# Low-rank inputs of an FFN folded into a redundant row of the quarter sums and into VectorE, with the next block's tokens turned between chunks

## The chip, the core and the metric

One core of a Trainium2 chip runs the whole program. The metric is the device time of one launch in microseconds (us). Before the change it is 2009.09 us, the median of three runs (2008.93 to 2010.6).

## What is computed

All tensors are float32. With x of shape (8, 256, 512), that is 2048 tokens of width 512:

```python
xn  = layernorm(x)                       # over the last axis
s   = attention(xn)                      # 128 heads, latent 64, rope 64
g   = silu(ffn(xn))
out = x + s * g

def qlora(x, wq, A, B):                  # r = 2
    return x @ tile(wq, (1, 4)).T + 0.5 * (x @ A.T @ B.T)
def ffn(x):
    gate = silu(qlora(x, w1q, a1, b1))   # w1q (1376, 128), a1 (2, 512), b1 (1376, 2)
    up   = qlora(x, w3q, a3, b3)
    return qlora(gate * up, w2q, a2, b2) # w2q (512, 344)
```

Since w1q is repeated four times along the inputs, x @ tile(wq).T is (the sum of x's four quarters) @ wq.T: a product over 128 inputs, not 512. To it comes a term of rank 2.

## The kernel before, in words

The program has two parts. `first_phase` computes the FFN's gate and the narrow projections of the attention; the second part is the attention with its output, in 64 units. Time between them is divided at 238 us of 2011. The change touches only `first_phase`.

The order of the work is written out by hand: each engine runs its instructions in the order of the program text, and waits on semaphores where data or a buffer is missing. A pool gives a tile a number of buffers for each tag; a new tile waits until an old one of the tag is released. All PSUM tiles come from one pool of eight banks of 128 x 512 (`bank`).

The FFN runs over four blocks of 512 tokens (`tb` 0 to 3). For each block:

- `norm` (L370) takes mean and variance on VectorE and finds 1/sqrt with Newton steps (VectorE in block 0, GpSimd in the others); `norm_rest` (L405) normalizes the four tiles of 128 tokens.
- `turn` (L414) transposes the tokens on TensorE, copies them out of PSUM alternately on ScalarE and VectorE, and sums the four quarters of the inputs, `xs`, with VectorE and GpSimd.
- `narrow` (L443) is the product with a13 and with the rotary key projection in one: rows 0, 1, 32, 33 (and copies at 64, 65, 96, 97) of `mid` are the rank-2 inputs of gate and up, the other rows go to DRAM.
- `down` (L453) is the product into the latent; its result and seven sums and differences of xn (`sum_x`, on GpSimd) go to DRAM for the attention.
- Six steps u of `low` and `main` make the 11 chunks of 128 hidden units, two at a time (step 5 has one). `low` (L466) starts each of the four banks of a step with the product of two rows of b13 and two rows of `mid` (K = 2, four row groups side by side); `main` (L478) adds the product over xs, takes Silu on ScalarE out of PSUM, and multiplies with up on VectorE into `hT`. `gate` and `hT` have two buffers each.
- `fold` (L498) sums the quarters of the hidden units on GpSimd, `low_out` (L512) makes the rank-2 term of the second layer in a bank `pm2` that is held over the block, `gate_out` (L536) is the last product, its Silu, and the store of the gate to DRAM by SP (`gs`, two buffers).

The next block's `norm` stands behind step 1, its `norm_rest` behind step 4, its `turn`, `narrow` and `down` behind step 5 and in front of `gate_out`. `between(0)`, behind `narrow(0)`, is `set_up` (L593 and on): SP loads two raw weights and a mask, GpSimd arranges them in 24 small copies and clears two value tiles, VectorE reduces the mask to `sides_sb`. `between(1)` and on, in blocks 2 and 3, load and compute the first units of the attention (`Project`, `Prepare`, `values`) between the steps of block 3.

`on_columns` (L168) writes a product as four matmuls of 32 columns that run side by side; each float32 matmul is two instructions in the profile.

Of the kernel before, what the change touches and what calls it, by code (L numbers as in the profile page):

```python
# [16 lines left out]
P = 128  # L17
# [7 lines left out]
TB = 512  # L25
# [12 lines left out]
def mla_ffn_gate_kernel(  # L38
# [42 lines left out]
    cs_d = [dram.tile([P, TB], F32, name=f"cs_d{n}") for n in range(NTB)]  # L81
    krs_d = [dram.tile([R, TB], F32, name=f"kr_d{n}") for n in range(NTB)]
# [221 lines left out]
    def first_phase(between):  # L304
# [8 lines left out]
        b13_sb = fw.tile([98, NCH, P], F32, name="b13_sb")  # L313
# [4 lines left out]
        xts, xns, xnT, xsum, mids = {}, {}, {}, {}, {}  # L318
# [8 lines left out]
        def load_chunks(to, of):  # L327

            of = of.rearrange("p (q f) -> p q f", q=4)
            nc.sync.dma_start(  # L330
                out=to[:, 0:8].rearrange("p (q n) m -> p q (n m)", q=4), in_=of[:, :, 0:256]
            )
            nc.sync.dma_start(out=to[:, 8:11, 0:88], in_=of[:, 0:3, 256:344])
            nc.sync.dma_start(
                out=to[:, 8:10, 96:128],
                in_=of[:, 3, 256:320].rearrange("p (m i) -> p m i", m=2),
            )
            nc.sync.dma_start(out=to[:, 10, 96:120], in_=of[:, 3, 320:344])

        for t in (w1_sb, w3_sb, b13_sb):  # L340
            nc.gpsimd.memset(t[:, 8:11, 88:96], 0.0)
            nc.gpsimd.memset(t[:, 10, 120:128], 0.0)
# [17 lines left out]
        nc.sync.dma_start(out=wdn_sb, in_=w_down.rearrange("(c p) m -> p c m", p=P))  # L360
        for n in range(2):
            for k in range(2):
                load_chunks(
                    b13_sb[64 * n + 32 * k : 64 * n + 32 * k + 2], b13[32 * k : 32 * k + 2, :]
                )
        load_chunks(w1_sb, w1t)
        load_chunks(w3_sb, w3t)
        load_x(1)

        def norm(tb):  # L370


            mv = f2.tile([P, 4, 2], F32, tag="mv", name=f"mv_{tb}")
            for n in range(4):
                s6 = f2.tile([P, 6], F32, tag="st", name=f"st_{tb}_{n}")
                nc.vector.bn_stats(s6, xts[tb][n])
                nc.vector.bn_aggr(mv[:, n, :], s6)
            ve = f2.tile([P, 4], F32, tag="ve", name=f"ve_{tb}")
            nc.vector.tensor_scalar_add(ve, mv[:, :, 1], EPS)
            i0 = f2.tile([P, 4], I32, tag="i0", name=f"i0_{tb}")  # L380
            nc.vector.tensor_single_scalar(i0, ve.bitcast(I32), 1, ALU.logical_shift_right)
            r0 = f2.tile([P, 4], I32, tag="r0", name=f"r0_{tb}")
            nc.vector.tensor_scalar(r0, i0, -1.0, float(0x5F3759DF), ALU.mult, ALU.add)
            r = r0.bitcast(F32)
            e = f2.tile([P, 4], F32, tag="e", name=f"e_{tb}")
            for step in range(3):
                new = f2.tile([P, 4], F32, tag=f"r{step}", name=f"r_{tb}_{step}")
                if tb == 0:
                    nc.vector.scalar_tensor_tensor(e, r, -0.5, r, ALU.mult, ALU.mult)
                    nc.vector.scalar_tensor_tensor(e, e, 1.0, ve, ALU.mult, ALU.mult)  # L390
                    nc.vector.scalar_tensor_tensor(new, e, 1.5, r, ALU.add, ALU.mult)
                else:
                    nc.gpsimd.tensor_mul(e, r, r)
                    nc.gpsimd.tensor_mul(e, e, ve)
                    nc.gpsimd.tensor_scalar(e, e, -0.5, 1.5, ALU.mult, ALU.add)
                    nc.gpsimd.tensor_mul(new, e, r)
                r = new

            off = f2.tile([P, 4], F32, tag="off", name=f"off_{tb}")
            if tb:  # L400
                nc.gpsimd.tensor_mul(off, mv[:, :, 0], r)
                nc.gpsimd.tensor_scalar(off, off, -1.0, None, ALU.mult)
            return mv, r, off

        def norm_rest(tb, mv, rstd, off):  # L405
            xns[tb] = xts[tb]
            for n, xn in enumerate(xts[tb]):
                one = rstd[:, n : n + 1]
                if tb:
                    nc.scalar.activation(xn, xn, AF.Identity, bias=off[:, n : n + 1], scale=one)  # L410
                else:
                    nc.vector.tensor_scalar(xn, xn, mv[:, n, 0:1], one, ALU.subtract, ALU.mult)

        def turn(tb):  # L414
            a = f1.tile([P, KT, TB], F32, tag="act1", name=f"act1_{tb}")
            xnT[tb] = a
            for n in range(4):
# [4 lines left out]
                if n % 2 == 0:  # L422
# [4 lines left out]
            xs = f2.tile([P, TB], F32, tag="xs", name=f"xs_{tb}")  # L427
            xs2 = f1.tile([P, TB], F32, tag="tmp", name=f"xs2_{tb}")
            nc.vector.tensor_add(xs, a[:, 0, :], a[:, 1, :])
            nc.gpsimd.tensor_add(xs2, a[:, 2, :], a[:, 3, :])  # L430
            nc.vector.tensor_add(xs, xs, xs2)
            xsum[tb] = xs

        def over_xn(tb, name, weights):
            ps = bank(f"{name}_{tb}")
            for cols in (ds(0, S), ds(S, S)) if name == "pm" and tb == 0 else (ds(0, TB),):
# [6 lines left out]
        def narrow(tb):  # L443
# [3 lines left out]
            mids[tb] = mid  # L447
# [11 lines left out]
        sets, hTs, h4s, mid2ps = {}, {}, {}, {}  # L459
# [6 lines left out]
        def low(tb, u):  # L466

            sets[tb, u] = []
            for i, c in enumerate(pair(u)):
                for k in range(2):  # L470
                    ps = bank(f"p{'xy'[k]}_{tb}_{u}_{i}")
                    r = slice(64 * i + 32 * k, 64 * i + 32 * k + 2)
                    nc.tensor.matmul(  # L473
                        ps, b13_sb[r, c], mids[tb][r], start=True, stop=False, skip_group_check=True
                    )
                    sets[tb, u].append(ps)

        def main(tb, u):  # L478
            n = u // 2
# [3 lines left out]
            for i, c in enumerate(pair(u)):  # L483
                px, py = sets[tb, u][2 * i : 2 * i + 2]
                on_columns(px, w1_sb[:, c], xsum[tb], False, True)
                on_columns(py, w3_sb[:, c], xsum[tb], False, True)
                gate = f2.tile([P, TB], F32, tag="gate", name=f"gate_{tb}_{u}_{i}")
                nc.scalar.activation(gate, px, AF.Silu)
                if c < 8:
                    nc.vector.tensor_mul(h[:, c // 2, :], gate, py)  # L490
                else:
# [4 lines left out]
                    )  # L496

# [52 lines left out]
        idle = bank("idle")  # L550
        for n in range(48):
            nc.tensor.transpose(idle[:, ds(n % 4 * P, P)], ident, ident)
        norm_rest(0, *norm(0))
        turn(0)
        narrow(0)
        between(0)
        for to, of in ((a2_sb, a2), (w2_sb, w2t), (w2_sb[96:98, 2, :], b2[0:2, :])):
            nc.sync.dma_start(out=to, in_=of)
        down(0)
        for tb in range(NTB):  # L560
            more = tb + 1 < NTB
            for u in range(6):
                low(tb, u)
                main(tb, u)
                if u in (2, 4):
                    fold(tb, u // 2 - 1)
                    low_out(tb, u // 2 - 1)
                if u == 1 and more:
                    stats = norm(tb + 1)
                if u == 4 and more:  # L570
                    norm_rest(tb + 1, *stats)
# [8 lines left out]
            if more:  # L580
                turn(tb + 1)
                low_out(tb, 2)
                narrow(tb + 1)
# [3 lines left out]
            gate_out(tb)  # L587

# [388 lines left out]
```

## Time and profile before

| | |
|---|---|
| median of 3 runs | 2009.09 us |
| the profiled execution | 2012.79 us |
| its span | 2011.0 us |
| granted TensorE clock, mean | 0.998 |
| `first_phase` up to the last pf matmul | 238.43 us |
| block 0 from the first px to the last pf | 21.73 to 70.99 us |
| L473, both groups | 176 instructions, 640 ns each, up to four at once |
| L490, products gate x up | 32, 687 ns each |

A line of the time line has start, length, engine, line of the program, operation, result<-inputs, shapes and count, and in brackets the idle time in front and what ended it. A line of the table by stages has start:end, length, then busy us and number of instructions of PE, PEld, DVE, ACT and POOL, the granted clock, the share of the DMA engines and GB/s. PE is TensorE, PEld its weight loads, DVE VectorE, ACT ScalarE, POOL GpSimd, SP the queue that issues the DMAs.

### The profile page before, as it was taken

The page shows a single profiled execution, that of the slowest core. Times are in us where ns is not written, and L with a number is a line of the kernel's source. Part 1 is how long each engine was busy: PE and PEld are TensorE (multiplying, and loading weights), DVE is VectorE, ACT ScalarE, POOL GpSimd, SP SyncE. Part 2 cuts the span into 40 slices and gives each one's busy share as a digit, 9 for nine tenths or more (in the row PEclk, how much of TensorE's full clock was granted, in tenths as well). Part 3 has the DMA queues.
Part 4 walks back from the last instruction along what each step waited for, and adds up shares of the span by engine and source line. Part 5 has one row for each costly group of instructions (what it writes and reads, how often), then busy time and mean ns, then how long its engine had stood idle before and what let it go on. Part 6 is the DMA issues. An engine that isn't in the chain of part 4 may idle for free.

```text
span 2011.0 us, 86602 instructions
## 1 busy us (share of the span) xinstructions
PE 1998.9 (99%) x38112; PEld 1412.7 (70%) x38112; DVE 1522.8 (76%) x2601; ACT 1079.4 (54%) x2958; POOL 725.9 (36%) x1076
## 2 busy tenths in 40 slices
PE   9999999999999999999999999999999999999998
PEld 4334577777777777777777767777777767777776
DVE  4332387878788777878787877878787877888788
ACT  2222365565556554555655645565565555556654
POOL 5445545545552323233233233223323323232231
PEclk9999999999999999999999999999999999999999
DMA  5233322222223223222223233222223222222212
GB/s 169 87 113 135 113 95 84 68 87 86 86 82 123 80 91 112 91 87 78 74 86 123 66 112 105 84 81 86 81 92 102 90 93 81 86 86 72 80 55 70
DMA packets 118188, 184.78 MB, mean 92 GB/s; under 512 B 10450, under 2 KB 84082, under 8 KB 117812
## 3 DMA queue, kind: packets, MB, share of 16 engines
q1 hardware_dynamic: 117812, 179.23, 26.4%
q8 instruction: 302, 4.95, 1.0%
q14 instruction: 74, 0.61, 0.1%
HBM read 145.12 MB, written 34.08 MB: 89 GB/s over the span
## 4 chain that ended last, share of the span: by engine, by line
PE 97%; DVE 2%; issue 0%; DMA 0%; ACT 0%; POOL 0%; SPq 0%; DVEq 0%
PE q L172 39%; PE sc L688 34%; PE av L734 11%; PE po L172 2%; PE pf L172 2%; PE px L172 2%; PE py L172 2%; PE px L473 1%; PE pm L172 1%; PE qq L250 1%; PE vps L285 1%; PE pp L172 1%; DVE pt L717 1%; DVE nmx L701 0%; PE pm L520 0%; PE xpt L420 0%
## 5 line engine op out<-in xcount | busy, mean ns | idle before, releaser
L707 ACT ACTIVATE pr<-sc,nmx 128x256 f32<-128x256 f32 x2048 | 816.5, 502 | 473.8 <-DVE nmx L701 471.0
L701 DVE TENSOR_REDUCE nmx<-sc 128x2 f32<-128x512 f32 x1024 | 635.6, 683 | 291.3 <-PE sc L688 267.4
L717 DVE STREAM_TRANSPOSE pt<-pr 128x512 f32<-128x512 f32 x1024 | 635.2, 678 | 0.0
L172 PE MATMUL q<-x,ws 128*32 128x256 f32 x8192 | 488.9, 379 | 0.6 <-POOL ws L136 0.6
L688 PE MATMUL sc<-act,qr 32*128 32x256 f32 x8192 | 489.0, 374 | 0.0
L215 POOL TENSOR_TENSOR e<-e,e 128x256 f32<-128x256 f32 x128 | 93.8, 733 | 1057.5 <-ACT e L210 570.6
L688 PEld LDWEIGHTS sc<-act,qr 32*128 32x128 f32 x8192 | 421.2, 185 | 22.2 <-issue 0.2
L172 PEld LDWEIGHTS q<-x,ws 128*32 128x32 f32 x8192 | 265.7, 110 | 177.2 <-POOL ws L136 1.1
L172 PE MATMUL q<-x,w 128*32 128x256 f32 x6144 | 381.5, 381 | 0.2 <-DMA w<-in_w_rope_dram 0.2
L172 PEld LDWEIGHTS q<-x,w 128*32 128x32 f32 x6144 | 186.9, 110 | 155.0 <-ACT pr L707 35.4
L688 PE MATMUL sc<-kc,qcm 32*128 32x256 f32 x4096 | 281.2, 387 | 0.0
L734 PE MATMUL av<-pt,vpad 128*32 128x128 f32 x8192 | 236.4, 273 | 1.9 <-ACT pr L707 1.2
L734 PEld LDWEIGHTS av<-pt,vpad 128*32 128x32 f32 x8192 | 226.3, 110 | 14.5 <-issue 3.0
L688 PEld LDWEIGHTS sc<-kc,qcm 32*128 32x128 f32 x4096 | 198.4, 184 | 52.1 <-issue 40.1
L210 ACT COPY e<-q 128x256 f32<-128x256 f32 x512 | 204.1, 399 | 27.9 <-PE q L172 26.3
L754 ACT ACTIVATE acc<-av,sides_sb 128x256 f32<-128x256 f32 (+1 forms) x130 | 54.3, 470 | 245.9 <-PE av L734 245.9
L270 POOL TENSOR_TENSOR qcm<-qc,mask_sb 128x1024 f32<-128x1024 f32 x64 | 122.3, 1911 | 9.6 <-ACT qc L260 9.6
L217 POOL TENSOR_TENSOR qr<-e,e 128x256 f32<-128x256 f32 x128 | 93.7, 732 | 10.0
L216 POOL TENSOR_TENSOR e<-e,e 128x256 f32<-128x256 f32 x128 | 93.5, 731 | 10.0
L227 DVE TENSOR_TENSOR qr<-e,q 128x256 f32<-128x256 f32 x128 | 53.9, 421 | 43.4 <-POOL e L215 24.4
L300 POOL COPY vpad<-vall 32x128 f32<-32x128 f32 x256 | 74.9, 293 | 14.8 <-ACT vall L292 4.4
L490 DVE TENSOR_TENSOR hT<-gate,py 128x512 f32<-128x512 f32 x32 | 21.5, 687 | 73.9 <-PE py L172 47.4
(105 smaller groups left out, 1107.4 us busy)
## 6 DMA issues: line engine op xcount, KB each, us to landing
w<-in_w_rope_dram SPq DMA_DIRECT2D x128, 512.0 KB
ws<-sums_d SPq DMA_DIRECT2D x96, 512.0 KB
sums_d<-ws SPq DMA_DIRECT2D x32, 512.0 KB
x<-xs_d SPq DMA_DIRECT2D x28, 256.0 KB
xt<-in_x_dram SPq DMA_DIRECT2D x16, 256.0 KB
xs_d<-xt SPq DMA_DIRECT2D x16, 256.0 KB
gate_d<-gs SPq DMA_DIRECT2D x16, 256.0 KB
g<-gate_d SPq DMA_DIRECT2D x16, 256.0 KB
```

What stands on the lines that cost most here:

```text
L172: nc.tensor.matmul(to[tile_], w[:, tile_], x, start=start, stop=stop, skip_group_check=True)
L210: nc.scalar.copy(self.e[i], self.banks[i])
L215: nc.gpsimd.tensor_add(m6, m6, m1)
L216: nc.gpsimd.tensor_add(m7, m7, m6)
L217: nc.gpsimd.tensor_add(self.out(1, 1), self.split(m7), self.split(m5))
L270: nc.gpsimd.tensor_mul(qcm, qks[b, sg // 2][0].rearrange("p (q i) -> p q i", i=32).unsqueeze(2).to_broadcast([P, 8, 4, 32]), mask_sb[:, ds ...
L300: nc.gpsimd.tensor_copy(vpad[rows, :, :, 8 * t + 4 * (sg % 2) :][..., :4], valls[b][rows, :, sg])
L688: nc.tensor.matmul(sc[r][:, h, :], lhs.rearrange("p t i -> p (t i)"), rhs, start=(part == 0 and h == 0), stop=(part == 2), skip_group_chec ...
L701: nc.vector.tensor_reduce(nmx[:, r, :], scs[n, f][r], AX.X, ALU.max, negate=True)
L707: nc.scalar.activation(p[:, h, :], scs[n, f][r][:, h, :], AF.Exp, bias=nmxs[n, f][:, r, h : h + 1])
L717: nc.vector.transpose(pts[n, f // 2, r].rearrange("p k q i -> p q k i")[:, ds(2 * (f % 2), 2)], prs.pop((n, f, r)).rearrange("p h (k j) -> ...
L734: nc.tensor.matmul(av[32 * r : 32 * r + 32, ds(half * P, P)], vpad[:, k, r, :], pt[r][:, k].rearrange("p q i -> p (q i)"), start=(k == 0), ...
```

## The change

The term of rank 2 no longer gets matmuls of its own (`low`, `b13_sb` are gone). Each half of it, one of the two ranks, takes another way.

The first rank goes through the main product. A column of the quarter sums has mean zero over all 512 inputs, so the 128 sums of quarters add up to zero: row 0 is minus the sum of the others. At the start w1 and w3 get their row 0 subtracted from all rows (`firsts`, ten K = 2 matmuls that spread the row over the partitions, their copies by ScalarE, and `less_first`), and row 0 then holds the first column of b13. The sums exist twice, `xs0` and `xs1`, and ScalarE copies row 0 or 32 of `mid` into row 0 of one of them.

The second rank is added by VectorE, in scalar_tensor_tensor instructions: the row of `mid` goes to DRAM (`low_d`) and comes back spread over all partitions (`low0`, `low1`); it is multiplied by a column of b13 (`bcol_sb`, turned on TensorE from `chunk_rows`) and added to the bank. For the gate the sum goes to SBUF, where Silu now works in place. For up it goes to `hT` for six chunks of a block from block 1 on, which GpSimd then multiplies, and otherwise back into the bank, from which VectorE multiplies.

Moved: `turn(tb + 1)` stands between steps 4 and 5; `norm` of block 2 and 3 stands behind the `gate_out` two blocks earlier, and the normalization goes one tile at a time behind steps 0 to 3 (in block 0, for block 1, behind steps 2 and 3); `low_out(tb, 0)` and `low_out(tb, 1)` stand behind steps 3 and 5 (before: 2 and 4); `narrow(tb + 1)` stands in front of `low_out(tb, 2)`; `between(0)` stands behind `gate_out(0)`. From block 1 on ScalarE makes all four copies of `turn`. The narrow product is in two halves in all blocks. The warming transposes at the start are 16, before 48.

```diff
-        b13_sb = fw.tile([98, NCH, P], F32, name="b13_sb")
+        bcol_sb = fw.tile([P, 16, 2], F32, name="bcol_sb")
...
+        rows = f1.tile([P, 3 * TB], F32, tag="h4", name="rows")[:, 0:F]
+        nc.scalar.dma_start(out=rows[64:97:32], in_=b13[0:33:32, :])
+        for k, wt in enumerate((w1t, w3t)):
+            nc.scalar.dma_start(out=rows[65 + 32 * k : 66 + 32 * k], in_=wt[0:1, :])
...
-                if n % 2 == 0:
+                if tb or n % 2 == 0:
                     nc.scalar.copy(a[:, 0:KT, ds(n * P, P)], pt)
...
+            xs = [f1.tile([P, TB], F32, tag=f"xs{k}", name=f"xs{k}_{tb}") for k in range(2)]
...
+            nc.scalar.copy(xs[1], xs[0])
...
+            nc.sync.dma_start(out=low_d[tb], in_=mid[1:34:32, :])
+            lows[tb] = []
+            for k in range(2):
+                t = f1.tile([P, TB], F32, tag=f"low{k}", name=f"low{k}_{tb}")
+                nc.sync.dma_start(out=t, in_=low_d[tb][k : k + 1, :].to_broadcast([P, TB]))
+                lows[tb].append(t)
+                nc.scalar.copy(xsum[tb][k][0:1], mid[32 * k : 32 * k + 1])
...
-        def low(tb, u):
...
-                    nc.tensor.matmul(
-                        ps, b13_sb[r, c], mids[tb][r], start=True, stop=False, skip_group_check=True
-                    )
...
         def main(tb, u):
...
+            for i, c in enumerate(chunks):
+                px, py = (bank(f"p{'xy'[k]}_{tb}_{u}_{i}") for k in range(2))
+                on_columns(px, w1_sb[:, c], xsum[tb][0], True, True)
+                on_columns(py, w3_sb[:, c], xsum[tb][1], True, True)
+                gates.append(f2.tile([P, TB], F32, tag="gate", name=f"gate_{tb}_{u}_{i}"))
+                ups.append((py, h[:, c // 2, :] if tb and c < 8 and (i == 0 or u in (0, 2)) else py))
+                nc.vector.scalar_tensor_tensor(
+                    gates[i], lows[tb][0], bcol_sb[:, place(c), 0:1], px, ALU.mult, ALU.add
+                )
+                nc.scalar.activation(gates[i], gates[i], AF.Silu)
+                nc.vector.scalar_tensor_tensor(
+                    ups[i][1], lows[tb][1], bcol_sb[:, place(c), 1:2], py, ALU.mult, ALU.add
+                )
+            for c, gate, (py, up) in zip(chunks, gates, ups):
+                if c >= 8:
...
+                elif up is py:
+                    nc.vector.tensor_mul(h[:, c // 2, :], gate, py)
+                else:
+                    nc.gpsimd.tensor_mul(up, gate, up)
...
+        def less_first(k, engine):
+            w_sb = (w1_sb, w3_sb)[k]
+            for c in (0, 4):
+                engine.memset(w_sb[0:1, c : c + 4], 0.0)
+                one = w_sb[:, c : c + 4]
+                engine.tensor_sub(one, one, firsts[k][:, c : c + 4])
...
         turn(0)
+        sums(0)
+        less_first(0, nc.gpsimd)
         narrow(0)
-        between(0)
+        less_first(1, nc.vector)
...
         for tb in range(NTB):
             more = tb + 1 < NTB
             for u in range(6):
-                low(tb, u)
                 main(tb, u)
-                if u in (2, 4):
+                if u in (3, 5):
                     fold(tb, u // 2 - 1)
                     low_out(tb, u // 2 - 1)
-                if u == 1 and more:
-                    stats = norm(tb + 1)
+                if u == 1 and tb == 0:
+                    stats = norm(1)
+                if more:
+                    for n in range(4):
+                        if u == (n if tb else 2 + n // 2):
+                            norm_one(tb + 1, n, *stats)
                 if u == 4 and more:
-                    norm_rest(tb + 1, *stats)
+                    turn(tb + 1)
...
             if more:
-                turn(tb + 1)
+                sums(tb + 1)
+                narrow(tb + 1)
                 low_out(tb, 2)
-                narrow(tb + 1)
                 down(tb + 1)
             else:
                 low_out(tb, 2)
             gate_out(tb)
+            if tb == 0:
+                between(0)
+            if tb + 2 < NTB:
+                stats = norm(tb + 2)
```

## The prediction

> **What bounds it now.** I read the busy shares and the chain that ended last first, then TensorE's time line, then the table by stage.
>
> ```profile
> PE 1998.9 (99%) x38112; PEld 1412.7 (70%) x38112; DVE 1522.8 (76%) x2601; ACT 1079.4 (54%) x2958; POOL 725.9 (36%) x1076
> ...
> PE 97%; DVE 2%; issue 0%; DMA 0%; ACT 0%; POOL 0%; SPq 0%; DVEq 0%
> ```
>
> TensorE is the chain, so a matmul less is time less, as long as nobody else becomes the bound. The stages:
>
> ```profile
> 21.73:70.99 49.26, 48.89 (x424) 15.86 (x420) 19.56 (x34) 14.80 (x23) 34.54 (x67) 1.00 0.42 141
> 70.99:122.48 51.49, 51.37 (x425) 16.44 (x421) 19.49 (x33) 13.90 (x23) 21.89 (x29) 0.97 0.31 106
> 122.48:170.70 48.22, 48.10 (x425) 15.54 (x421) 19.59 (x33) 14.01 (x23) 27.57 (x37) 1.00 0.31 102
> 170.70:238.43 67.73, 67.73 (x952) 29.63 (x949) 14.98 (x25) 19.93 (x42) 35.18 (x43) 1.00 0.32 110
> ```
>
> These are token blocks 0 to 3 (length, then PE, PEld, DVE, ACT, POOL busy, granted clock). After 238.43 each engine's instructions stand in the same order in both programs, so the 1772.6 us of attention keep their time. All is decided in the first 238 us. VectorE is busy for under 20 of some 50 us per block: room, but not boundless.
>
> **What is removed.** Per step u, L473 lies between 21.73, its first row, and 22.80, the first product row: 1.07 us. Six steps in four blocks: 24 x 1.07 = 25.7 us, 6.4 per block. The narrow product in halves costs 0.05 us a block (3.48 against 3.43 in whole). If nothing else bound: 2009.1 - 25.5 = 1983.6.
>
> **What is added on VectorE.** 22 scalar_tensor_tensor per block, one input in PSUM. The nearest rows:
>
> ```profile
> L532 DVE SCALAR_TENSOR_TENSOR h<-pm,h 32x512 f32<-32x512 f32 x12 | 8.3, 691 | 1.4 <-ACT h L530 1.0
> L431 DVE TENSOR_TENSOR xs<-xs,xs 128x512 f32<-128x512 f32 x4 | 6.0, 1490 | 11.0 <-POOL xs L430 11.0
> ```
>
> L431 (both inputs in SBUF) takes 1.76 us at 59.39, where GpSimd works, and 0.69 at 17.48, where it has just begun a memset. The Trainium skill, "SBUF — State Buffer", Terms, says that VectorE and GpSimd lock one port pair for a whole instruction and the loser blocks fully. Taken for every instruction, GpSimd busy half of the time would add about 0.5 x 1.07 us to 22 instructions: 12 us a block, and the change would lose. But the three L532 from 61.18 to 63.3 take 0.71 each beside GpSimd's uninterrupted subtractions (59.3 to 64.8). The new instruction has L532's form, so the row decides. I take 0.72, between 0.69 and 0.75, which L446 takes with a pointer scalar: 15.8 us a block. The subtractions in less_first(1) have two SBUF inputs and pay 1.75.
>
> **Start (to 21.7).** The ten new K=2 matmuls take about 5.5 us at L473's 0.5 to 0.69 per pass. They lie in front of the transposes, which wait for VectorE's normalization until 11.17 (2.9 us idle before): nothing, unless the row loads are over 2 us late. The clock was half from about 10.7 to 14.6 and the 16 transposes took 3.6 instead of 2.0; with less idle there up to 1.4 us may be gained. Bounds -1.4 to +1; taken: 0.
>
> **Edits costed at nothing.** The two row copies into the sums and the copy of the sum, on ScalarE (0.59 each by L530): they end about 2.5 us after mid; the next main product comes 3.4 (pp) or 15 us (pp, low_out, pf) after it; uncovered, 2.5 a block. less_first(0) on GpSimd (17.4 to about 22.8): the first product needs only its first subtraction, over by about 19.4, under pp. It delays sum_x(0), whose results SP stores while nothing waits. All four transposed copies on ScalarE (0.59 against VectorE's 0.65) and the normalization one tile at a time between Silus (0.73 to 0.80, L410): ScalarE is busy for 14 of 50 us; if they came late, turn(tb+1) would hold TensorE, 1 to 2 us a block. Turning before step 5 takes four banks while pm2 holds one: in blocks 1 and 2 VectorE empties banks at the rate of the products, so under 1 us, within the 0.8 and 1.5 below. On SP w1 and w3 come about 8 us earlier, since 16 loads of b13 give way to six behind them: early enough for the first product at 21.7, too. low_d and its two broadcasts stand in front of kr_d, cs_d and xs_d and hold SP for the first landing; the 3.4 below counts that. In blocks 2 and 3 the broadcasts have 10 us of pf to land in. The transpose of chunk_rows (0.3 us on TensorE) and its copy lie under the wait for the low rows.
>
> **Block 0: VectorE becomes the bound.** Its products stay on VectorE: 22 x 0.72 + 14 x 0.69 (L490, L493, L494) + 4.0 for the statistics (32.40 to 36.38) + 1 for waits on Silu = 30.5 us, where TensorE needs about 26 to the same point. It can't begin before the low-rank rows have been to DRAM and back. mid ends at 19.2 (18.44 + 0.75); two DMAs in series, about 5 us by the 3 to 4.5 of other landings, with less_first(1) alongside: 25.5. So the last product is at 56.0. Then TensorE alone: low_out 1.7, pp 3.4, pf 10.4, and 0.5 for half clock: 72.0, against 70.99. The 6.4 us are spent: +1.0.
>
> **Block 1: the moved set-up.** set_up now stands behind gate_out(0) on SP, GpSimd and VectorE, in front of block 1. Its parts as they were:
>
> ```profile
> 29.68 0.16 DVE L617 TENSOR_REDUCE sides_sb<-mask_sb 128x2 f32<-128x8 f32 x1 [10.49 <-DMA mask_sb<-in_kmask_dram]
> ...
> 27.48 0.41 POOL L611 COPY wup_sb<-raw 128x64 f32<-128x64 f32 x2 [9.57 <-DMA raw<-in_w_up_dram]
> ...
> 35.46 0.90 POOL L623 MEMSET vpad<- 32x128 f32 x4
> ...
> 75.95 1.21 ACT L546 ACTIVATE gs<-pf 128x512 f32<-128x512 f32 x2 [5.95 <-DMA gate_d<-gs]
> ...
> 71.50 6.01 SPq L547 DMA_DIRECT2D gate_d<-gs  x4
> ```
>
> In block 0 those waits cost nothing: TensorE ran ahead over eight banks. Now: the last product (56.0) + rest of the fold 2.8, xs2 1.3, sum 1.76, mid 0.75 gives mid at 62.6. SP reached gate_d 7.4 us after mid (64.1 to 71.50); the trip of the low rows stands in front, 3.4: 73.4. Third and fourth gs wait for the first gate_d to land, so SP is held 6.0: 79.4. raw and mask take 2.9 to issue: 82.3; mask lands 2.5 later (the row allows 3.7): 84.8. VectorE, waiting for mask, then does block 2's statistics, 4.0: 88.8. Meanwhile raw lands at 82.9, GpSimd copies and clears for 8.9 (27.48 to 36.36), then does the Newton steps, 3.9 (41.51 to 45.39): 95.7, and only then the first gate product, 1.3: 97.0. There are two gate tiles, so step 1's first addition waits for that. Queued behind it are all of VectorE's additions, and for those TensorE waits, its eight banks full at about 80. From 97.0 VectorE has 18 x 0.72 + 8 x 0.69 + 0.8 = 19.3 left: 116.3; TensorE's tail 15.5: 131.8. Block 1 takes 59.8, against 51.5: +8.3. Bounds: +4 if every landing takes 2 us, +13 if each takes 4.5.
>
> Half clock: the skill, "TensorE: Matmul & The Clock Gate", Part 1, lets the clock fall after an idle window of about 3.4 us. The trace is stricter: 1.6 us of bank waits (75.6 to 78.3) were followed by
>
> ```profile
> 80.00:82.00 2.00, 2.00 (x12) 0.50 0.30 111
> ```
>
> and 1.7 us lost. By the rule only block 1's stall lowers the clock, by the row also block 0's small waits. Both fall where VectorE is the bound and TensorE has slack; hence only 0.5 above. If the half clock reached the tails: 1.7 more in each of blocks 0 and 1.
>
> **Block 2.** With six products on GpSimd, VectorE has about 22 us of work in 26 us of TensorE: TensorE bound again. gate_d lands 4 to 5 us into the block (124.0 before), which holds ACT, then Silu, then a gate tile until 7.5: with 19.3 more that is 26.8, against TensorE's 26.3. 48.2 - 6.4 + 0.8 = 42.6: -5.6.
>
> **Block 3.** The matmuls of the projections (four times 6.2 us) give VectorE slack. GpSimd, busy 35.2 of 67.7, gets 6 x 1.3 = 7.8 more, less the moved sum; in-order waits between products, sum_w and joins, and later loads of x: 1.5 taken (0 to 4). -6.4 + 1.5 = -4.9.
>
> **Sum.** +1.0 + 8.3 - 5.6 - 4.9 = -1.2 us against the profiled execution, 2012.79 (span 2011.0, 1.8 around it). The median of the runs is 2009.09; the difference carries over: 2007.9. A measurement of this kernel tells about 0.2%, 4.0 us, from no change.
>
> **Rivals.**
> (A) As worked out: most of 25.7 us is given back, two thirds of that in block 1. 2008, own range 2002 to 2013. 0.50.
> (B) The set-up hides: raw and mask land early and GpSimd is done before its products are needed. Block 1 then takes about 43: -8.5 instead of +8.3, 1991. For it: GpSimd was idle from 64.8 to 88.3. Against it: three landings in series on SP and 13 us of in-order GpSimd work behind them. Half-hidden cases reach 2003. 0.17.
> (C) Slower: the addition itself is dearer on VectorE. Block 0 and the rest of block 1 hang on it with 22 and 18, block 2 has only 0.5 us of slack and then 18: about 6 us for each 0.1 us. Over 0.2% slower from 0.81 us; at 0.85, 2015; were it to block like L431, far beyond. For it: 0.75 at L446, waits between Silu, GpSimd and VectorE over only two gate tiles; against: L532. 0.33.
>
> **Chances.** Faster: B and a low A, 0.27. Within: 0.40. Slower: C, 0.33. Range 2000 to 2018: it cuts B's early part and C's far end.
>
> **What would show it.** The additions near 0.72. TensorE idle some 10 to 17 us between about 80 and 97, ended by VectorE, behind it GpSimd's gate product and the set-up's copies. Block lengths near 50, 60, 43, 63. VectorE over 60% busy in block 0. An attention part of 1772.6. I am wrong if block 1 is under 50, if blocks 2 or 3 are not shorter than before, or if the attention part moves.

## The result, and the profile after

The changed kernel takes 2015.71 us (median of 7 runs, 2012.38 to 2017.05) beside 2009.5 us for the kernel before (7 runs, 2008.93 to 2010.6): ratio 1.0027, interval 1.0015 to 1.0039. It is slower. A second comparison, with 13 runs of the changed kernel, gave 1.0018 (1.0010 to 1.0026). The forecast was "no change", at 2008.

The profiled execution of the changed kernel took 2013.68 us (span 2011.9), 2 us less than its median. First the busy times from the page after, then the shares of the chain that ended last:

```profile
PE 1980.9 (98%) x38021; PEld 1407.9 (70%) x38021; DVE 1575.8 (78%) x2673; ACT 1093.7 (54%) x2987; POOL 756.1 (38%) x1107
...
PE 90%; DVE 3%; POOL 3%; issue 1%; DMA 1%; SPq 1%; ACT 0%; POOLq 0%; ACTq 0%; DVEq 0%
```

TensorE has 18 us less work, but the chain, 97% TensorE before, now leaves it for VectorE, GpSimd, SP and DMA. The table by stages shows where. Block 0 runs from its first px (the first bank of a gate product) to its last pf (the block's last product), each later block from the end of the one before it.

```profile
22.63:69.98 47.35, 43.45 (x413) 14.40 (x416) 37.18 (x58) 17.77 (x29) 28.42 (x37) 0.96 0.37 128
69.98:130.52 60.54, 46.80 (x413) 14.98 (x408) 34.11 (x59) 17.24 (x28) 37.12 (x69) 0.86 0.29 98
130.52:173.17 42.65, 41.38 (x413) 14.65 (x408) 26.67 (x37) 17.02 (x28) 29.32 (x35) 1.00 0.37 125
173.17:239.75 66.58, 62.73 (x908) 28.65 (x900) 26.33 (x41) 19.47 (x42) 48.10 (x57) 0.97 0.39 137
```

Block 1 is 9 us longer than before, though it has less to do: TensorE idles 13.7 us of it and the granted clock is 0.86. Blocks 0 and 2 are 2 and 5.6 us shorter, block 3 only 1.2. What is left behind block 3 takes 1772.1 us, 0.4 less than before. The stall of block 1 in the time line after, all engines, a few lines of it:

```profile
84.23 0.16 DVE L720 TENSOR_REDUCE sides_sb<-mask_sb 128x2 f32<-128x8 f32 x1 [17.99 <-DMA mask_sb<-in_kmask_dram]
88.87 0.22 DVE L421 TENSOR_SCALAR r<-i 128x4 int32<-128x4 int32 x1
89.12 0.75 DVE L532 SCALAR_TENSOR_TENSOR gate<-low,bcol_sb,px 128x512 f32<-128x512 f32 x1
89.93 1.93 PE L173 MATMUL px<-xs,w_sb 128*32 128x512 f32 x8 [8.83 <-DVE gate L532]
91.83 0.20 POOL L431 TENSOR_TENSOR e<-r 128x4 f32<-128x4 f32 x1
95.68 2.50 POOL L549 TENSOR_TENSOR hT<-gate,hT 128x512 f32<-128x512 f32 x2
95.75 0.81 ACT L448 ACTIVATE xt<-xt,off,r 128x512 f32<-128x512 f32 x1 [3.90 <-POOL off L441]
96.99 0.75 DVE L532 SCALAR_TENSOR_TENSOR gate<-low,bcol_sb,px 128x512 f32<-128x512 f32 x1 [5.14 <-POOL hT L549]
```

VectorE stands 18.0 us for the mask, then does block 2's statistics, whose last result (L421) comes at 89.1; its first addition of the block comes at 89.12. GpSimd ends its set-up at 91.8 and begins the Newton steps (L431). Its first product comes at 95.68, behind them, and the third gate's addition at 96.99 waits for it. ScalarE's normalization of block 2's tokens (L448, at 95.75) waits for the last Newton step (L441). The product and the normalization begin within 0.1 us of each other; the experiments had to tell the two paths apart.

Block 3 in the same view:

```profile
179.12 1.23 ACT L599 ACTIVATE gs<-pf 128x512 f32<-128x512 f32 x2 [7.01 <-DMA gate_d<-gs]
181.09 2.53 POOL L549 TENSOR_TENSOR hT<-gate,hT 128x512 f32<-128x512 f32 x2 [13.02 <-ACT gate L535]
189.40 1.90 POOL L271 TENSOR_TENSOR qcm<-qc,mask_sb 128x1024 f32<-128x1024 f32 x1
191.26 1.28 POOL L549 TENSOR_TENSOR hT<-gate,hT 128x512 f32<-128x512 f32 x1
192.57 0.75 DVE L532 SCALAR_TENSOR_TENSOR gate<-low,bcol_sb,px 128x512 f32<-128x512 f32 x1 [6.65 <-POOL hT L549]
195.27 1.18 ACT L211 COPY e<-q 128x256 f32<-128x256 f32 x4
195.68 1.79 PE L173 MATMUL q<-x,w 128*32 128x256 f32 x24 [2.74 <-ACT e L211]
```

Read it downwards as a chain. ScalarE waits 7.0 us for a gate store of block 2 to land, so the Silus behind it are late, so GpSimd makes two products at 181.09 and then runs what stands next in its queue, the weight sums and the spread, for 7.7 us. Its third product ends at 192.5, only then is a gate free for VectorE, and ScalarE, which takes its instructions in order, copies the projections' banks (L211) after the Silus that waited. TensorE finds no bank for 2.74 us.

### The profile page after: what moved, and what is told of

Read it like the earlier page. It is cut to its first block, busy times and chain, and to the rows that moved or that the text cites. A ratio compares the mean times of both kernels' runs of the same rounds, so it can differ in the third digit from the quotient of the medians.

```text
span 2011.9 us, 86607 instructions
## 1 busy us (share of the span) xinstructions
PE 1980.9 (98%) x38021; PEld 1407.9 (70%) x38021; DVE 1575.8 (78%) x2673; ACT 1093.7 (54%) x2987; POOL 756.1 (38%) x1107
## 4 chain that ended last, share of the span: by engine, by line
PE 90%; DVE 3%; POOL 3%; issue 1%; DMA 1%; SPq 1%; ACT 0%; POOLq 0%; ACTq 0%; DVEq 0%
PE q L173 39%; PE sc L791 34%; PE av L837 11%; PE po L173 2%; PE qq L251 1%; DVE pt L820 1%; PE vps L286 1%; PE pf L173 1%; POOL h4b L562 1%; PE px L173 0%; DVE nmx L804 0%; POOL hT L549 0%; POOL h L561 0%; PE py L173 0%; POOL h L563 0%
## 5 line engine op out<-in xcount | busy, mean ns | idle before, releaser
L211 ACT COPY e<-q 128x256 f32<-128x256 f32 x512 | 203.5, 399 | 21.5 <-PE q L173 20.2
L173 PE MATMUL px<-xs,w_sb 128*32 128x512 f32 x352 | 50.3, 644 | 14.4 <-DVE gate L532 11.9
```

The source lines that it names most:

```text
L173: nc.tensor.matmul(to[tile_], w[:, tile_], x, start=start, stop=stop, skip_group_check=True)
L211: nc.scalar.copy(self.e[i], self.banks[i])
```

## The experiments

All are edits of the changed kernel. "First px" and the blocks are from each run's profile; the median and the ratio to the kernel before (with its 95% interval) from its timed runs.

| run | first px | blocks 0, 1, 2, 3 (us) | median | ratio |
|---|---|---|---|---|
| before | 21.73 | 49.3, 51.5, 48.2, 67.7 | 2009.5 to 2010.7 | 1 |
| changed | 22.63 | 47.4, 60.5, 42.7, 66.6 | 2015.71 | 1.0027 (1.0015-1.0039) |
| e11 changed again | 23.91 | 46.8, 60.9, 42.7, 65.3 | 2014.12 | 1.0018 (1.0010-1.0026) |
| e1 set-up back | 22.58 | 54.6, 43.7, 43.3, 66.5 | 2006.53 | 0.9984 (0.9978-0.9991) |
| e2 reduction late | 24.22 | 47.0, 60.2, 42.9, 64.5 | 2014.20 | 1.0019 (1.0012-1.0025) |
| e3 block 3's products on VectorE | 26.37 | 46.8, 60.6, 42.7, 63.8 | 2011.57 | 1.0002 (0.9996-1.0009) |
| e4 = e1 + e3 | 26.25 | 54.7, 44.1, 42.9, 61.7 | 2003.10 | 0.9968 (0.9955-0.9980) |
| e5 = e4 + e2 | 25.23 | 50.9, 43.7, 43.0, 61.8 | 1997.06 | 0.9939 (0.9927-0.9952) |
| e6 no first matmuls | 20.15 | 46.4, 59.5, 42.6, 66.2 | 2008.03 | 0.9990 (0.9982-0.9998) |
| e7 first matmuls with 128 rows | 25.05 | 45.1, 60.4, 43.2, 66.4 | 2013.14 | 1.0015 (1.0008-1.0021) |
| e8 = e5 without additions | 24.20 | 52.3, 41.0, 40.7, 60.6 | 1992.02 | 0.9912 (0.9897-0.9927) |
| e9 GpSimd's set-up in pieces | 22.53 | 44.9, 51.6, 41.1, 62.0 | 1999.33 | 0.9948 (0.9935-0.9960) |
| e10 two-row control to e7 | 25.75 | 47.1, 60.6, 42.7, 64.8 | 2015.57 | 1.0030 (1.0021-1.0039) |
| e12 = e2, all products on VectorE | 24.57 | 46.8, 59.3, 44.0, 62.0 | 2011.21 | 1.0000 (0.9992-1.0008) |
| e13 = e2, Newton before the set-up | 26.55 | 46.6, 56.9, 42.0, 66.7 | 2012.44 | 1.0005 (0.9998-1.0012) |
| e14 = e13, all products on VectorE | 26.74 | 46.6, 46.4, 43.7, 61.6 | 1999.14 | 0.9941 (0.9929-0.9954) |
| e15 set-up behind the token sums | 25.02 | 47.6, 44.0, 42.4, 62.3 | 1994.59 | 0.9922 (0.9909-0.9936) |
| e16 = e15 without additions | 26.29 | 47.9, 41.2, 40.7, 60.6 | 1990.45 | 0.9899 (0.9886-0.9913) |

### The set-up, first round: e1, e2, e3, e4

e1 puts the set-up back where the kernel before has it:

```diff
         narrow(0)
+        between(0)
         less_first(1, nc.vector)
...
-            if tb == 0:
-                between(0)
```

> The set-up of the second phase (mask, raw weights, GpSimd's copies and memsets, the reduction of the mask on VectorE) goes back to where it stood, behind the narrow product of block 0; all else is the changed kernel. Set-up theory (the stall of block 1 is GpSimd's set-up and VectorE's wait for the mask): block 1 falls from 60.5 us to 44-47, block 0 gets 0-3 longer (the first additions stand behind the mask's landing), blocks 2 and 3 stay at 42.6 and 66.7; total 11-15 us below the changed kernel, 2001-2005, so below the kernel before. Dear-additions theory (VectorE's 22 additions a block are the bound whatever else is queued): block 1 stays above 55, total within 4 us of the changed kernel.

Block 1 fell by 16.9 us, to 43.7: the set-up theory. The median, 2006.53, stayed above the 2001 to 2005 expected, because block 0 grew by 7.3, not 0 to 3: `less_first(1)` stands on VectorE behind the reduction, which waits for the mask until 29.95, and TensorE waited 7.9 us for the corrected weights.

e2 moves only the reduction of the mask on VectorE to block 1, behind step 3:

```diff
+                if u == 3 and tb == 1:
+                    nc.vector.tensor_reduce(
+                        sides_sb, mask_sb.rearrange("p (n e) -> p e n", e=2), AX.X, ALU.add
+                    )
...
-        nc.vector.tensor_reduce(
-            sides_sb, mask_sb.rearrange("p (n e) -> p e n", e=2), AX.X, ALU.add
-        )
```

> Only the reduction of the mask on VectorE is taken out of the set-up and put into block 1 behind its fourth step; GpSimd's part of the set-up stays at the end of block 0. If GpSimd's queue is what holds block 1 (its products come behind its copies, and the gates come free by its products): the first additions come 4-8 us sooner (80-85 instead of 89), the third gate's addition still waits to about 95-97, block 1 stays at 58-60.5, total 0-2 us lower. If VectorE's wait for the mask alone is the stall: block 1 falls to 47-51, total 9-13 us lower.

The first additions of block 1 came 17 us sooner (72.2 against 89.1; 4 to 8 were expected), and block 1 still took 60.2. Taking away the 18 us for the mask, VectorE's longest wait in this part of the program, gained almost nothing, since GpSimd's queue holds the block without it. It does not follow that the wait is harmless: the Newton steps need VectorE's statistics, which ended at 89.1, only 2.7 us before GpSimd was free for them. With GpSimd's set-up gone and the mask's wait left, block 1 would by these two numbers gain about 2.7 us, an estimate; no run has the mask's wait alone.

e3 gives block 3's GpSimd products to VectorE:

```diff
-                ups.append((py, h[:, c // 2, :] if tb and c < 8 and (i == 0 or u in (0, 2)) else py))
+                ups.append((py, h[:, c // 2, :] if 0 < tb < NTB - 1 and c < 8 and (i == 0 or u in (0, 2)) else py))
```

> In block 3 alone the six products that GpSimd makes go to VectorE, which reads the banks directly, as in block 0. If block 3 loses its 4 us because GpSimd's products stand between the sums of weights and the spread, so that gates come free late and ScalarE's copies of the projections stand behind the Silus: block 3 falls from 66.7 to 62-63.5 and the total by 3-5 us. If VectorE is the bound there, or the late landing of the rows for ScalarE's gate stores is: block 3 stays within 1 us, total the same. Blocks 0 to 2 as in the changed kernel in both cases.

Block 3 took 63.8, 2.7 us less, and the median fell by 2.6 to 4.1. Block 3 varies from profile to profile, but the two groups do not overlap: 64.5 to 66.7 in the eight profiles of the table with GpSimd's products there, 61.6 to 63.8 in the seven with the additions and without those products. So the products in GpSimd's queue are a cause of the loss; the order of the chain above, through ScalarE to TensorE, is read from the time line.

e4 has both edits.

> The set-up back behind the narrow product of block 0, and block 3's GpSimd products on VectorE. If the two stalls are separate, their gains add: 14-19 us below the changed kernel, 1997-2002, so 8-12 us below the kernel before. If they share a cause (VectorE too full), the sum is less than the larger of the two plus 1 us.

The gains add (9.2 and 4.1 us in the medians singly, 12.6 together), below the range of 14 to 19 by what e1 loses in block 0.

### Two paths through GpSimd's queue: e12, e13, e14

e12 is e2 with the products of all blocks on VectorE, so that no product stands behind the set-up.

> The set-up stays at the end of block 0 as the change put it, only the reduction of the mask stands in block 1 behind its fourth step; but no product is GpSimd's: in all four blocks VectorE makes them from the banks. If block 1's stall is GpSimd's products that stand behind its set-up: block 1 falls from 60.5 to 44-47, block 2 stays within 1.5 us of 42.6, block 3 61-63.5; total 1994-2000. If VectorE then has too much (22 additions, 14 products and the statistics in a block): blocks 1 and 2 at 46-50, total above 2003.

This expectation failed: block 1 kept 59.3 us. ScalarE's time line in e12 names the second path:

```profile
80.16 1.15 ACT L535 ACTIVATE gate<-gate 128x512 f32<-128x512 f32 x2
97.03 0.81 ACT L448 ACTIVATE xt<-xt,off,r 128x512 f32<-128x512 f32 x1 [15.72 <-POOL off L441]
97.75 1.13 ACT L535 ACTIVATE gate<-gate 128x512 f32<-128x512 f32 x2
```

The normalization of the next block's first tile stands between two pairs of Silus and waits 15.7 us for GpSimd's Newton steps, which stand directly behind the set-up there (from 93.14). All Silus behind it wait as well. So e13 puts `norm(2)` ahead of the set-up, and e14 does that with all products on VectorE:

```diff
+            if tb + 2 < NTB:
+                stats = norm(tb + 2)
             if tb == 0:
                 between(0)
-            if tb + 2 < NTB:
-                stats = norm(tb + 2)
```

> The statistics and reciprocal root of block 2's tokens are put ahead of the set-up at the end of block 0, and the reduction of the mask behind block 1's fourth step; GpSimd's products stay. If GpSimd's products behind its set-up hold block 1 as well: the third gate comes free when the set-up ends, at 92-94, 3-4 us sooner than in the changed kernel, block 1 takes 56-58.5 and the total falls 2-5 us (2010-2013). If the reciprocal root that ScalarE waits for is the only path: block 1 falls to 44-48, total 1999-2003.

> As the run with the reciprocal root ahead of the set-up, and all products on VectorE in every block, so that nothing of block 1's first half stands behind the set-up on GpSimd but its folds. If the two paths are all: block 1 falls to 44-48 (the first fold comes behind the set-up at about 92-94, as its first halves are due at 92), block 3 stays at 62, total 1995-2000. If there is a third path behind the set-up: block 1 stays above 52, total above 2003.

Block 1 and the total came as expected in both. Block 1 of e13 and of e14:

```profile
73.17:130.11 56.94, 43.90 (x413) 14.49 (x408) 30.05 (x49) 16.99 (x28) 37.88 (x72) 0.88 0.31 106
73.37:119.74 46.37, 42.30 (x412) 17.13 (x408) 32.98 (x55) 17.00 (x28) 30.03 (x64) 1.00 0.38 127
```

With the Newton steps free and the products still behind the set-up, block 1 takes 56.9; with the products free and the Newton steps behind it (e12), 59.3; with both free, 46.4. Either path alone is enough to hold block 1. GpSimd's part of the set-up stood where the change put it in all three; the mask's reduction was out of the way in all three.

### A place for the set-up: e5, e9, e15

e5 is e4 with the reduction late, so that GpSimd's part and the transfers stand in block 0 and `less_first(1)` waits for nothing.

> The set-up's transfers and GpSimd part stand behind the narrow product of block 0, but the reduction of the mask stands in block 1 behind its fourth step, and block 3's products are VectorE's. In the run with only the set-up put back, block 0 took 54.6 us (7.3 more than the changed kernel's), with TensorE waiting 7.9 us for the last weight correction that stood on VectorE behind the reduction. If that order on VectorE is the whole price: block 0 returns to 47-48.5, block 1 stays at 43-45, block 2 at 42.6-43.3, block 3 at 61-63; total 1994-1998. If GpSimd's copies in block 0 cost by themselves (its sums of the tokens and folds come late): block 0 50-53, total 1999-2002.

1997.06: below both kernels and within the first forecast, but block 0 took 50.9, as the second one said. ScalarE waited 6.9 us for the Newton steps of block 1's tokens, and TensorE 4.4 us for those tokens. e9 deals GpSimd's part out to the six steps of block 1.

> As the run with the set-up split and block 3's products on VectorE, but GpSimd's part of the set-up is dealt out to block 1: one piece (about 1.2 to 1.8 us of copies, or one padding tile's memsets) behind each of its six steps; the transfers are still issued behind the narrow product of block 0. In the run that had all of it in block 0, ScalarE stood 6.9 us in front of a token's normalisation, for GpSimd's reciprocal root that came behind the set-up and the token sums. If that was the 3 us by which its block 0 stayed above the changed kernel's: block 0 falls from 50.9 to 47-48, block 1 stays within 1 us of 43.7, total 1993-1996. If block 0's extra came from its late start and clock alone: block 0 stays at 50-51, total 1996-1999.

Block 0 fell, to 44.9, further than expected, but block 1 rose to 51.6, and with it the total to 1999.33, neither as expected: the pieces push the folds and the token sum behind them (L471 at 105.3), and the last product waits 5.7 us for the rank-2 part (L585). e15 issues the transfers behind `narrow(0)` and puts GpSimd's part behind block 0's token sums, where GpSimd was idle for 10.3 us in the changed kernel (`between(0)` now only issues transfers, `parts` are the copies and memsets):

```diff
         narrow(0)
+        between(0)
...
         down(0)
+        for n in range(6):
+            parts[n]()
```

> The set-up's transfers stand behind the narrow product of block 0, GpSimd's copies and memsets behind block 0's token sums (in the 10 us in which GpSimd waits for the next block's statistics in the changed kernel), the reduction of the mask in block 1; block 3's products are VectorE's. If the place costs nothing: block 0 45-47.5, block 1 43.5-45, block 2 42.5-43.5, block 3 61-62.5, total 1992-1996. If GpSimd's copies slow VectorE or ScalarE beside them, or push the reciprocal root: block 0 at 49 or more, total at 1997 or more.

All four blocks came within their ranges or under 0.15 us outside. 1994.59 us, ratio 0.9922 (0.9909 to 0.9936), 15 to 16 us below the kernel before, is the best version found that computes the whole function:

```profile
25.02:72.66 47.64, 43.55 (x413) 14.23 (x416) 40.97 (x68) 17.75 (x29) 35.95 (x70) 0.96 0.42 141
72.66:116.61 43.95, 41.88 (x412) 14.48 (x408) 29.91 (x49) 17.01 (x28) 29.32 (x35) 1.00 0.35 120
116.61:158.98 42.37, 41.38 (x413) 14.67 (x408) 26.40 (x37) 17.01 (x28) 34.26 (x43) 1.00 0.40 134
158.98:221.26 62.28, 61.12 (x908) 41.41 (x900) 30.22 (x47) 19.77 (x42) 35.73 (x44) 1.00 0.41 142
```

In block 1 GpSimd now has 29.3 us of work instead of 37.1 and the clock is full.

### The price of the additions: e8, e16

Both leave out all additions (e8 from e5, e16 from e15). With them GpSimd's products in blocks 1 and 2 go to VectorE, so the difference holds both.

> As the run with the set-up split and block 3's products on VectorE, but all 88 additions of the low-rank terms are left out (the gates and second factors lack their low-rank part beyond what the redundant row carries), and all products are VectorE's, straight from the banks. The difference to that run is the whole price of the additions, with their waits for the broadcast rows. If VectorE has room for them: 1-4 us, most of it in block 0. If they are too dear: 8 us or more, in all four blocks.

> As the run with the copies behind the token sums, with all 88 additions of the low-rank terms left out (gates and second factors lack their low-rank part beyond what the redundant row carries), all products on VectorE from the banks. The earlier pair gave 2.7, 2.3 and 1.1 us for the additions in blocks 1, 2 and 3. If they cost the same here and 1-3 us in block 0: the total is 6-9 us below its pair, 1985-1989. If their price was mostly another stall: less than 4 us.

The medians differ by 5.0 and 4.1 us (the intervals of each pair touch or just overlap; both pairs agree). Blocks 1, 2 and 3 lose 2.7, 2.3, 1.1 us in the first pair and 2.8, 1.7, 1.7 in the second; block 0 none, since there the other waits stay (in e8 ScalarE stands 13.9 us for the Newton steps). So the additions cost about 2 us in each of blocks 1 to 3: more than "room enough" (1 to 4 in all), less than "too dear" (8 or more), and the 6 to 9 expected of e16 was too much.

### The start: e6, e7, e10, e11

e6 leaves out the first matmuls (ten, 20 instructions in the profile; the expectations call them sixteen) and the weight corrections, and has the 48 warming transposes again.

> The sixteen matmuls that work out the redundant row, their copies, and the correction of both weights by it are left out (so the first row's part of the quarter sums is not replaced), and the 48 transposes of the kernel before stand at the start again; all else is the changed kernel. Start theory (the few-row matmuls at the start do not hold TensorE's clock and push the first transposes; how much depends on where the clock's 3.4 us windows fall): the first product starts at 21.7-22.2 us in every run, no half clock between 15 and 22; with the corrections gone the first addition comes 2-3 us sooner in block 0; total 3-6 us below the changed kernel, its runs within 3 us of each other. If the start is no cause of the slower and more scattered runs: the same scatter of about 5 us and a total within 2.5 us of the changed kernel.

The first product starts at 20.15, sooner than expected, and the median is 6 to 8 us below the changed kernel's, more than the 3 to 6 expected. Of the profiled difference, 2.5 us are the start and about 1 each blocks 0 and 1. e6 does not separate the first matmuls from the corrections, which are gone with them. Its runs still scatter (2005.9 to 2011.5), so the start is not the whole scatter. e7 lets the ten matmuls read 128 rows, all but two of them zero; e10 has the same clearings and two rows.

> The same sixteen matmuls read all 128 rows, of which all but two are zeros (one clearing of the rows on VectorE and a clearing of the other operand on GpSimd are added); the result is the same. If it is the number of rows that lets the clock fall, they run at full clock to about 11-12 us, there is no half clock between 9 and 16, the first product starts at 21.8-22.8, total 1.5-3 us below the changed kernel with less scatter. If the rows do not matter (the clock follows something else): half clock in the start as before, first product between 22.6 and 27, total within 1 us of the changed kernel or higher by the added clearing.

> The control to the run with 128-row first matmuls: the same clearings and waits, but the sixteen matmuls read two rows again. There they ran from 9.2 to 16.1 us, the clock rose at 12.2 and stayed, and the first product started at 25.05. If the few rows keep the clock down: the matmuls take 9-10 us (to about 18.5), the clock rises only with the transposes behind them, the first product starts at 27-29, total 2-4 us above that run (2015-2017). If the number of rows does not matter: the first product at 24.5-25.5 and the total within 1 us of it.

TensorE alone by 3 us stretches (busy us, instructions, granted clock, DMA). In e7, where the matmuls ran from 9.19 to 16.06:

```profile
7.00:10.00 3.00, 0.81 (x1) 0.80 1.06 270
10.00:13.00 3.00, 3.00 (x8) 0.63 0.78 212
13.00:16.00 3.00, 3.00 (x16) 1.00 0.21 39
16.00:19.00 3.00, 3.00 (x41) 1.00 0.84 275
```

In e10, where they ran from 6.47 to 14.45:

```profile
7.00:10.00 3.00, 3.00 (x11) 0.82 1.06 274
10.00:13.00 3.00, 3.00 (x5) 0.50 0.75 209
13.00:16.00 3.00, 3.00 (x14) 0.50 0.23 64
16.00:19.00 3.00, 3.00 (x22) 0.50 0.85 278
```

TensorE is busy in every stretch of the second table, and its clock falls to half at 8.9 and stays there until 19.2; in the first it is idle from 5.0 to 9.19 and at full clock 3.0 us after the 128-row matmuls begin. Two-row matmuls do not hold the clock. e7 gains little in time by it, since its matmuls begin only at 9.19 (4.96 in the changed kernel): its first px came at 25.05, where 21.8 to 22.8 had been expected. e10 was 2.4 us slower than e7 in the median, as expected, though its first px (25.75) was not as late as expected; its matmuls began at 6.47.

e11 is the changed kernel once more.

> The changed kernel as it is, once more, for a second profile and more timed runs. In the first profile the run took 2013.7 us with the first product at 22.6, 2 us under the median of its runs. If the start's clock windows make that difference: time less the start of the first product is again 1991 within 1.5 us, whatever the start, and the median is again 2014-2016. If the start is not it: the first product is again at 22.6 within 0.5 us while the time differs by 2 us or more.

Time less first px was 1989.3 against 1991.1, 1.8 us apart where at most 1.5 was expected: this run started later and still took 0.5 us less, so the start alone does not set the time. Block 3 was 1.2 us shorter, without the half clock that followed TensorE's wait in the first profile. Fourteen profiles (those of the table without before, e6, e7 and e10) have the same TensorE work up to the first px. They reach it between 22.5 and 26.7, median 24.8: the first matmuls end anywhere from 11.4 to 15.2, by how many of them run at half clock. In eight of the fourteen the clock fell to half between 7.4 and 9.1, in the midst of the two-row matmuls; in the other six the first matmuls took 9.8 us, and no full clock is on record before 17.6. The Trainium skill, "TensorE: Matmul & The Clock Gate", Part 1, says that the clock follows a free-running activity window of about 3.4 us, so that the same kernel meets it in another phase each run; the traces agree (every half-clock stretch on record is 3.4, 6.8, 10.2, 13.7 or 17.1 us long, one to five times 3.41). It also says that a busy window raises the clock; these traces show that being busy with two rows does not.

## Why the prediction was wrong, point by point

- **The sign.** Against its own profiled execution the sum was off by 2.1 us: forecast -1.2, measured +0.9 (2013.68 less 2012.79). That it came so near is partly luck: block 0 was 2.9 us too pessimistic and block 3 3.8 us too hopeful. Against the medians it was off by 7.7. Three steps failed: the start taken at 0, block 3's waits taken at 1.5, and "the difference carries over". The profile of before lies 3.3 us above the median of its 7 runs (2.1 to 2.6 above the medians of 25 to 57 runs in the later comparisons), that of after 2.0 below its own. For the profile of after the start is a part of it. The nearest thing to a test of the start's term is e6, without the first matmuls and the corrections: its median, 2008.03, is where the forecast was, though with a first px 1.6 us sooner than forecast, so this too is partly chance.
- **Start: "taken: 0".** The first px came at 22.63 in the profile, at 24.8 in the median of fourteen: +0.9 and about +3. "They lie in front of the transposes" and cost "nothing" took the matmuls' durations at full clock (5.5 us). They take 6.5 to 9.8, since they run at half clock for part or all of the way, and push the transposes by up to 4 us. The bounds (-1.4 to +1) were too narrow.
- **Additions at 0.72.** Busy 0.744 (44 at L532), one every 0.66 while nothing is waited for. The prediction was right not to apply the port rule of the Trainium skill to every instruction. That page, "SBUF — State Buffer", limits it itself ("Who interferes with whom"): an instruction of VectorE with at most one input in SBUF, outside its two-port modes, does not contend with GpSimd. The trace agrees: none of the 88 additions took over 0.76, while L472, with two inputs in SBUF, took 1.75 beside GpSimd. A dearer addition, rival C's mechanism, is thus not what made the kernel slower, though its sign came true. The price of having the additions is about 2 us in each of blocks 1 to 3 (e16), of which block 2's forecast had 0.8.
- **Block 0: forecast 50.3 long, measured 47.4.** Right in kind (VectorE busy 79% of the block), 3 us too pessimistic. The additions began at 27.6, not 25.5, since VectorE's weight corrections lasted until then. But VectorE needed 27.5 us to its last product instead of 30.5 (22 times 0.06 for the spacing of 0.66 are 1.3, the waits for Silu, 1.0, did not come, and the rest is the products and statistics), and what TensorE has left behind it took 1.1 less.
- **Block 1: forecast 59.8, measured 60.5; the gate free at 97.0, measured 96.99.** Right, down to the chain through the mask, the raw weights and GpSimd. Incomplete in one point: the second path, ScalarE's normalization behind the Newton steps, was not seen. It ends at the same time, so the sum did not suffer, but a remedy read off the forecast, moving the products, gains almost nothing in this block (e12).
- **Block 2: forecast 42.6, measured 42.65.** Right.
- **Block 3: forecast 62.8, measured 66.6.** This is the term that was mis-sized in the profile: "in-order waits between products, sum_w and joins: 1.5 taken (0 to 4)" measured 5.3 with the half clock behind it (4.0 in e11, without it). e3 and e4 bring the block to 63.8 and 61.7. The wait was named; that ScalarE's order turns it into a wait of TensorE's projections was not.
- **Attention part: 1772.6 forecast, 1772.1 measured.** Right.
- **Rival B** (a hidden set-up, 1991) was not the outcome, but it was the version to look for: e15, 1994.6.

With the usual start and the mean of the changed kernel's two profiles the differences are: start +3.1, blocks -2.2, +9.3, -5.6 and -1.8, and -0.6 behind them, some 2.2 us above the profile of before. That is 2015.0, beside medians of 2014.1 and 2015.7. What stays open is why the profile of before lies above its medians: there is only one, and a part of the 3.5 to 6.2 us between the medians of the two kernels is just this distance. Nor is it shown why the two profiles of the changed kernel differ by 1.8 us behind their first px; block 3 holds 1.2 of it.

## What to carry to other kernels

When a step is moved in a hand-ordered program, list for each queue it enters everything that stands behind it, and ask of each item who waits: here both the products and twelve tiny Newton steps stood behind 24 copies on GpSimd, and either was enough. Removing the longest wait need not gain anything (18 us of VectorE for the mask: 0.3 us of block 1) while other queues hold the same work; each path's part showed only when the others were out of the way (e12, e13, e14). And a forecast of a few microseconds made from one profiled execution is no better than that execution's distance from its median, above all where, as here, the clock decides how long the start takes.

## What the hardware showed unexpectedly

- Two-row matmuls keep TensorE busy in the records for 8.0 us (e10) at half clock from 8.9 on. In e3 and e4 they last 9.8 us; there the clock is on record only from 20.1 and 19.9, at full, and the transposes behind the matmuls took 3.67 us, as in e10 at half clock (1.94 in e7 at full). The clock rises 2.8 to 5.4 us after matmuls or transposes with 128 rows begin (e3, e4, e5, e7, e10).
- In the changed kernel's profile, waits of TensorE of 2.6 us (block 1, to 77.7) and 2.7 us (block 3, to 195.7) each came with a stretch of half clock of 3.4 us (from 77.3 and from 196.8). The 1.6 us of waits that the prediction read in the kernel before lie in a stretch of 2.6 us (75.7 to 78.3) in which TensorE has only two-row matmuls. That such a stretch counts like a wait is inferred from e10, not tested.
